# A residual chain of four conditioned layers: the due times of every operation, and thirty unread products, set anew

## The chip, the core and the metric

The kernel runs on one core of one Trainium2 chip. The time is device time in microseconds (us) of one execution; the program is run several times, and the median of the runs is compared. The core has five engines with a queue of instructions each: TensorE (PE, with weight loads shown as PEld), VectorE (DVE), ScalarE (ACT), GpSimd (POOL) and SyncE (SP, which here only issues transfers). Each queue is worked off in its own order; an instruction waits on semaphores for the results that it needs.

## The reference, cut to what matters

The input `x` has 128 sequences of 64 tokens of 256 features in float32, 8192 tokens in all. Four layers are added to it one after the other, each steered by a condition vector of its sequence:

```python
x = x + L0(x, cond)   # keys = values = queries = modulated linear of x; per token, softmax over
                      # the 16 heads' 16-wide keys; modulated linear out
x = x + L1(x, cond)   # per-sequence 256->64->256 with relu, and its own residual
x = x + L2(x, ids, …) # layer norms with gathered gains, three small MLPs of the conditions,
                      # concatenation (6*256) @ int_W1, silu, @ int_W2, layer norm
x = x + L3(x, cond)   # per-sequence 256x256 weight of rank 30: x @ (U @ V) + bias
```

The softmax runs over heads within a token, so the scores of a token are 16 x 16. Everything that depends on conditions alone (styles, demodulations, the decoded `U` of rank 30, the bias rows of the three MLPs) is worked out once.

## The kernel before, in words

The tokens are cut into 16 blocks of 512 (8 sequences each), with features on the partitions in most steps. A prologue (`prologue_keys`, `prologue_rest`, block number -1 in the tables) works out what depends on conditions alone. Its loads are those at lines 702 to 709 (`early`, `wk` 704, `idx` 705, `sel` 706, `wo` 707, `kbr` 708, `late` 709), 642 and 647 (weights and tables), 842 (`wd`, pieces of `W_dec`); its products are at line 629 (small ones) and 851 (decoding `W_dec`, copied on by DVE at 866 or ACT at 858).

Each block has `attention` and `rest`:

- xsT = xT times the style (POOL, 1097; `xT` is loaded at 1039, the token ids at 1044, their one-hot rows `oh` are made by DVE at 1046).
- For each of two pairs: keys (PE, 1191, 8 matmuls), kxe (DVE 1202, POOL 1213), transposes kT and kV (DVE 1228 and 1245), kR (ACT 1237), v (PE 1256, ACT 1261), scores into `sc` (PE 1276, 128 matmuls), maxima (DVE 1289), mt (ACT 1302), a product (PE 1311), mX (ACT 1321), mE (DVE 1328, 1337), the shift of the scores (PE 1350), exponentials e (ACT 1364), the weighted values (PE 1381, 128 matmuls), ao (DVE 1394), rz (DVE 1402), att (POOL 1405), a turn (PE 1418), osT (DVE 1425).
- The output product (PE 1155) and x1T (DVE 1162, 1173).
- L1: PE 1573 and 1591, DVE 1604, with per-block weights from POOL (1129 to 1143). L2: transposes (PE 1648), statistics (DVE 611, 613), rstd (POOL 619, 621; offset by DVE 1623), normalizations (ACT 1633), transposes (PE 1688, ACT 1693), picks (PE 1699, 1716), the large product (PE 1738, sixteen pieces and two of line 1748, between which other work can go), tanh (ACT 1755), DVE 1758, the second product (PE 1785, DVE 1796). L3: PE 1823, 1842, 1867, DVE 1874, output by SP at 1883. The last block ends in `finish` (lines 1447 to 1557), which works in halves.

PSUM is divided into one tile `sc` of four banks and four single banks, which nearly every product takes and gives back when its result was read.

The order on each engine is not that of the program text. Every operation is recorded in a plan with a due time, and the plan is emitted by due time as far as dependences and free buffers allow:

```python
def turns(blk, k):                                   # line 573
    return max(blk, 0) * TURN + tables[blk][k]
...
o["prio"] = self.turns(o["blk"], o["k"])             # in Plan.order
...
o = ops[heappop(ready)[1]]                           # the ready operation that is due first
```

`TURN` is 881500 in units of 1/20000 us, that is 44.1 us from block to block, so work of three or four blocks is interleaved on each engine. `TURNS` holds one table of due times for the prologue and one for each block. The plan also decides which slot of a buffer kind, and which PSUM bank, an operation gets.

The prologue's table has more entries than the prologue has operations. What is left over becomes unread products, made by `spin`: a bf16 product of zeros of 128 x 512, whose result nobody reads. It occupies PE and takes a PSUM bank:

```python
def spin():                                          # line 634
    ps = Buf("bank")
    pe(0.215, lambda: nc.tensor.matmul(ps.t, idle[:, :128], idle, start=True, stop=True), [], [ps], n=2)
...
while plan.noted[-1] + 1 < SPINS:                    # line 1897; SPINS is the length of the prologue's table
    spin()
```

Before, there are 23 of them: 7 at the start, 4 ahead of the last block's product of line 1573, 7 in `finish` behind line 1447, and 5 by themselves.

Of the kernel before, what the change touches and what calls it, by code (L numbers as in the profile page):

```python
# [66 lines left out]
class Plan:  # L67
# [98 lines left out]
    -652225 -652207 -501809 -501797 549383 103302 97834 98988 -85347 -290328 36942 -280951 36928 -327022 -327038  # L166
    -295554 -34519 99192 -93568 76051 -488538 -331376 250663 -320110 311371 -544127 -297616 224193 -331358 437866
    369544 404601 258598 475097 427655 312750 413551 304934 313766 312765 477842 -325751 561445 451452 460137 631735
    653018 914561 435225 761948 708892 413433 313012 683513 477384 477856 415801 449087 706556 405021 840033 397966
    837121 677936 790176 413437 1085501 936816 1219990 374944 1127563 -488523 52290 364768 79632 -329221 31806 69353  # L170
    -302391 37394 74911 -302398 -135690 103317 253823 37375 113108 263257 -19093 -550935 407657 459732 455180 631946
    302035 554215 632190 302064 695445 435656 1285010 1313672 -271895 459095 641073 632445 439004 715974 662881
    443771 715988 735063 451708 763102 706553 455767 763114 790156 408270 1002127 1127290 1030643 1260783 1163421
    1039496 1260792 1322499 1326714 1592341 1603338 1296229 962570 1143817 400034 1095103 400034 1114596 1105723
    370540 1181851 589031 1073580 1215404 1215398 420508 1317621 426029 1244494 1155098 517782 411678 1318626
    1221030 487418 1289492 1063938 409314 1219811 414916 1426329 1505888 1316718 425996 578876 1307095 1544800
    1509955 1509945 1500478 1779993 1762953 1714110 1556735 1872029 1343778 1433951 1901071 1540726 1505870 1355549
    1749223 1065262 1886158 1894341 1920839 1713830 1294728 1463917 2023267 2025009 2024993 1769125 2080980 1991910
    1476886 1764730 2069423 1404270 2200384 1433935 1923896 1907021 2044892 1919551 2192488 1893429 2159446 1342047
    1346981 1402219 2313495 2045469 2494753 2285999 2271380 2543401 2525610 1728898 1728909 2630317 2592995 1746037  # L180
    2451743 1728921 2595973 1718576 1277644 2062908 2395255 316359 450207 16049267 16049281 14504150 -291503
    11290964 2389482 -291825 16049286 -291820 14522440 16049266 16053420 -320001 13567795 -410994 14513815 -361547
    15405911 16048186 16073369 -309973 14522440 16005249
    """,
    0: """
    -484581 84372 -652203 -35682 684863 1289506 1005368 578863 1258365 2419509 2111364 2061858 1597541 357479
    -327047 377451 733801 366553 -328204 806711 387288 365083 406034 1377907 1111313 1160718 1672215 -332266 56194
    404606 447219 455369 431572 -15187 267150 595783 567747 302041 312750 629212 662899 609068 653445 312737 466428
    715978 309121 309112 857128 436276 489161 370548 806701 1063944 1120732 641246 410676 725568 436305 410648
    709812 410662 609042 1119259 602370 436294 477217 820104 818673 1002143 818654 1083255 1103114 1063941 1120265  # L190
    1117581 1073560 1181852 1168792 409321 1262701 1205334 414910 1357801 1505886 426004 1063898 411662 1462748
    1518640 1230468 1433890 1749255 1749239 1431873 1872425 2190164 1919575 1872422 2174910 2278764 2321415 2384852
    2430654 2088493 2292286 2543835 2599889 2409496 1589520 2271367 2543830 2512135 1803634 1326310 2714126 1751071
    1758943 1758957 1758947 2523186 1589506 2427752 2206922 2711663 1788133 2711694 1788156 2575469 2528666 2544499
    2733360 2898539 2917556 2711682 2568763 2598822 2598852 2711679 2711696 2733311 2598849 2781651 2986041 2354176
    2409591 2568757 2598832 2711671 2711680 2733358 2733329 2733335 2985571 2986044 2476838 3049866 2529124 3019122
    3049851 2529112 3092405 3152898 3152886 2477574 3204028 3204039 2342116 2350219 3160743 3160731 2697860 3153889
    3310393 3353979 3296818 3367447 3109127 3394993 3420441 3762300 1336203 3409996 1469597
    """,
    1: """  # L200
    -394079 -394092 -482733 -425615 -297831 -337865 -325537 -299039 -482716 297196 735637 407985 -421370 1532404
# [1818 lines left out]
```

## Time and profile before

| what | value |
|---|---|
| median of 9 runs (lowest, highest) | 824.1 us (816.78, 828.93) |
| profiled execution: time, span | 818.67 us, 816.8 us |
| mean granted TensorE clock over the span | 0.980 |
| busy: PE, PEld | 753.3 us (92%), 488.4 us (60%) |
| busy: DVE, ACT, POOL | 591.4 us (72%), 360.8 us (44%), 565.5 us (69%) |
| transfers | 87.63 MB, mean 107 GB/s |
| queue of instruction loads (q8) | 101 packets, 1.65 MB |

Busy time is the sum over an engine's instructions in one profiled execution. The granted clock is the share of full speed at which TensorE was let run. "Idle before" names the time an engine stood still ahead of an instruction, and what ended it; "issue" means that the profile shows nothing that the engine waited for. The chain of waits is followed back from the last instruction, at each step to what released it.

### The profile page before, as it was taken

Reading aid. Unit: us, or ns where it says so; the run is one execution under the profiler, and the core shown is the slowest. Engines: PE = TensorE matmul, PEld = TensorE weight load, DVE = VectorE, ACT = ScalarE, POOL = GpSimd, SP = SyncE. Lnnn points to the kernel's source line nnn. Section 1 sums busy time; section 2 is a strip of 40 time slices with the busy share of each in tenths; the row PEclk is TensorE's granted clock in tenths of the full one; section 3 lists DMA queues with packets and bytes.
Section 4 is the critical chain, followed back from the end, with each engine's and each line's share of the span. In section 5 each row is a group of like instructions: output and inputs, shape, how many; then the busy total and the mean of one; then the engine's idle time right before and its main releaser. Section 6 shows DMA issues by size and latency. Waiting matters only on the chain.

```text
span 816.8 us, 29440 instructions
## 1 busy us (share of the span) xinstructions
PE 753.3 (92%) x12839; PEld 488.4 (60%) x12843; DVE 591.4 (72%) x1320; ACT 360.8 (44%) x664; POOL 565.5 (69%) x544
## 2 busy tenths in 40 slices
PE   8777889999999999999999999999999989999595
PEld 5655665666666565666666666657566565655353
DVE  4748896968778696969587786869695876866435
ACT  1554345543635362635435353636254353444331
POOL 5453869395868879586869688786779486828243
PEclk9997999999999999999999999999999999999888
DMA  8876742233423244342424333342434232023001
GB/s 269 253 228 205 216 132 85 73 105 107 130 94 81 75 111 119 91 127 85 122 88 107 116 86 106 96 122 68 130 83 123 72 83 63 3 68 99 18 1 53
DMA packets 59297, 87.63 MB, mean 107 GB/s; under 512 B 6456, under 2 KB 42400, under 8 KB 59168
## 3 DMA queue, kind: packets, MB, share of 16 engines
q1 hardware_dynamic: 54048, 68.96, 28.8%
q0 software_dynamic: 5120, 16.78, 7.3%
q8 instruction: 101, 1.65, 0.9%
q14 instruction: 28, 0.23, 0.1%
HBM read 72.48 MB, written 13.24 MB: 105 GB/s over the span
## 4 chain that ended last, share of the span: by engine, by line
PE 61%; DVE 21%; POOL 7%; ACT 5%; issue 4%; DMA 1%; SPq 0%; DVEq 0%; POOLq 0%; ACTq 0%
PE bank L1738 24%; PE bank L1191 6%; PE bank L1785 5%; DVE st L611 4%; DVE mr L1289 4%; PE sc L1276 3%; PE bank L1688 3%; PE bank L1381 3%; PE bank L629 2%; DVE bank L1162 2%; PE bank L1573 2%; PE bank L851 2%; PE bank L1648 1%; PE bank L1823 1%; ACT e L1364 1%
## 5 line engine op out<-in xcount | busy, mean ns | idle before, releaser
L1289 DVE TENSOR_REDUCE mr<-sc 128x16 f32<-128x1024 f32 x64 | 75.7, 1210 | 9.9 <-PE sc L1276 9.9
L1364 ACT ACTIVATE e<-sc 128x1024 f32<-128x1024 f32 x64 | 62.3, 1026 | 33.6 <-PE sc L1350 33.5
L1112 POOL DMA_INDIRECT pw<-in_pw,idx x64 | 65.3, 1021 | 16.0 <-issue 8.2
L1155 PE MATMUL bank<-osT,wo 128*128 128x512 f32 x128 | 63.8, 627 | 5.4 <-DVE osT L1425 5.1
L1738 PE MATMUL bank<-uu,w_s 128*128 128x512 f32 x128 | 63.3, 597 | 0.0
L1191 PE MATMUL bank<-wk,xsT 128*128 128x256 f32 x256 | 62.2, 386 | 0.9 <-DVE uu L866 0.5
L1237 ACT ACTIVATE kR<-kT,early 128x1024 f32<-128x1024 f32 x32 | 39.7, 1242 | 50.0 <-DVE kT L1228 50.0
L1738 PE MATMUL bank<-uu,w_t 128*128 128x512 f32 x128 | 61.3, 605 | 0.3 <-ACT uu L1655 0.2
L1738 PE MATMUL bank<-uu,w_h 128*128 128x512 f32 x128 | 61.4, 602 | 0.0
L1738 PE MATMUL bank<-x2T,w_x 128*128 128x512 f32 x128 | 59.9, 593 | 0.0
L1276 PEld LDWEIGHTS sc<-kR,kT 20*64 20x64 f32 x4096 | 47.5, 130 | 20.0 <-ACT e L1364 8.3
L1381 PEld LDWEIGHTS bank<-e,v 64*32 64x32 f32 x4096 | 44.6, 107 | 24.2 <-issue 20.2
L1785 PE MATMUL bank<-w,uu 128*128 128x256 f32 x240 | 55.8, 385 | 2.2 <-DVE uu L1758 2.1
L1276 PE MATMUL sc<-kR,kT 20*64 20x64 f32 x4096 | 52.3, 232 | 4.6 <-ACT e L1364 1.7
L1381 PE MATMUL bank<-e,v 64*32 64x64 f32 x4096 | 51.0, 230 | 5.8 <-issue 5.8
L1191 PEld LDWEIGHTS bank<-wk,xsT 128*128 128x128 f32 x256 | 48.4, 196 | 12.5 <-issue 3.6
L1202 DVE TENSOR_TENSOR kxe<-bank,dmk 128x512 f32<-128x512 f32 x32 | 22.0, 688 | 43.8 <-PE bank L1191 38.5
L1693 ACT COPY uu<-bank 128x512 f32<-128x512 f32 x64 | 36.4, 587 | 36.4 <-PE bank L1688 36.1
L1785 PEld LDWEIGHTS bank<-w,uu 128*128 128x128 f32 x240 | 44.3, 190 | 9.8 <-DVE uu L1758 3.8
L1129 POOL TENSOR_TENSOR wdn<-gdb,late 128x512 f32<-128x512 f32 x32 | 40.6, 1281 | 13.0 <-PE bank L1573 12.0
L1228 DVE STREAM_TRANSPOSE kT<-kxe 128x512 f32<-128x512 f32 x64 | 42.1, 685 | 9.3 <-POOL kxe L1213 9.3
L1213 POOL TENSOR_TENSOR kxe<-kxe,kbr 128x512 f32<-128x512 f32 x32 | 40.8, 1274 | 10.5 <-DVE kxe L1202 10.2
(241 smaller groups left out, 1783.9 us busy)
## 6 DMA issues: line engine op xcount, KB each, us to landing
xT<-in_xT SPq DMA_DIRECT2D x32, 256.0 KB
gdb<-dgdb SPq DMA_DIRECT2D x16, 512.0 KB
ubb<-ugub SPq DMA_DIRECT2D x32, 256.0 KB
wup<-ugub SPq DMA_DIRECT2D x32, 256.0 KB
ids<-in_ids SPq DMA_DIRECT2D x16, 256.0 KB
ud<-uu SPq DMA_DIRECT2D x8, 512.0 KB
uT<-ud SPq DMA_DIRECT2D x16, 256.0 KB
dmk<-demod_k SPq DMA_DIRECT2D x60, 64.0 KB
```

Of the source, the lines that this page charges most:

```text
L1112: lambda tl=tl, n=n: nc.gpsimd.indirect_dma_start(out=pw[tl // 2].t[:, tl % 2, :], out_offset=None, in_=a["pw"], in_offset=bass.IndirectOf ...
L1129: lambda w=w, dp=dp: nc.gpsimd.tensor_tensor(w(), gdb.t[:, :, 0:64], dp, ALU.mult),
L1155: nc.tensor.matmul(ps.t, owT[:, c, bass.ts(oc, 128)], osT.t[:, c, :], start=(c == 0), stop=(c == C - 1))
L1191: nc.tensor.matmul(ps.t[:, bass.ts(l, F)], xsT.t[:, c, mine2].rearrange("p (n l) -> p l n", l=2)[:, l, :], kwT[:, c, :], start=(c == 0), s ...
L1213: lambda: nc.gpsimd.tensor_tensor(kxe.t[:, :, :, 0:D], kxe.t[:, :, :, 0:D], heads(kinds["kbr"][0]).unsqueeze(1).to_broadcast([128, 2, H, D ...
L1228: lambda l=l: nc.vector.transpose(kT.t[:, l, :].rearrange("p (g h t) -> p h g t", h=H, t=QT), kxe.t[:, l, :, :]),
L1276: nc.tensor.matmul(sc.t[64 * c : 64 * c + 64, q, bass.ts(tg, 64)], cut(kT.t)[r, tg // 4, c, tg % 4, :], cut(kR.t)[r, tg // 4, c, tg % 4, : ...
L1289: lambda two=two: nc.vector.tensor_reduce(mr.t[:, two, :], sc.t[:, two, :].rearrange("p q (g n) -> p q g n", g=TG), AX.X, ALU.max),
L1364: lambda k=k: nc.scalar.activation(es[k].t, sc.t[:, 2 * k : 2 * k + 2, :], AF.Exp, scale=0.25),
L1381: nc.tensor.matmul(placed(pr[c].t)[32 * q : 32 * q + 32, l, g, :, :], v.t[r, l, :].rearrange("p (g q d) -> p g q d", g=4, q=4)[:, g, q, :] ...
L1738: lambda ps=ps, w=w, src=src, fc=fc, c=c, n=n: nc.tensor.matmul(ps.t, w.t[:, c, bass.ts(fc, 128)], src.t[:, c, :], start=(n == 0 and c == ...
L1785: nc.tensor.matmul(ps.t[:, bass.ts(l, F)], s2.t[:, c, bass.ts(2 * p + l, 128)], w2.t[:, c, :], start=(c == 0), stop=(c == C - 1),)
```

## The change

Only numbers change: `TURN` stays, the 16 tables of the blocks keep their lengths, and the prologue's table grows from 254 to 261 entries, which makes 30 unread products of 23. All other code is the same, so every other operation is there once, with the same operands.

```diff
 TURNS = {
     -1: """
-    -652225 -652207 -501809 -501797 549383 103302 97834 98988 -85347 -290328 36942 -280951 36928 -327022 -327038
...
+    -677219 -677238 -664467 -664429 538934 -664462 85946 87100 -161988 -331753 -149704 -321377 -161974 -294788
...
     0: """
-    -484581 84372 -652203 -35682 684863 1289506 1005368 578863 1258365 2419509 2111364 2061858 1597541 357479
...
+    -406988 84372 -652203 -27393 684863 1289506 1054617 1026520 1054613 1243452 2073912 1311799 1606077 355488
...
     15: """
...
 }
 SPINS = len(TURNS[-1].split()) if -1 in TURNS else 331
```

Both programs were built, and their queues laid side by side. Without the unread products, so many operations of each engine stand at the same place in its queue as before:

| engine | operations | at the same place | largest move (places) |
|---|---|---|---|
| PE | 851 | 661 | 9 |
| DVE | 894 | 633 | 19 |
| ACT | 640 | 423 | 11 |
| POOL | 532 | 339 | 7 |
| SP | 348 | 167 | 13 |

Most moves are an exchange of two neighbours, such as two of the sixteen pieces of line 1738, two of the four normalizations of line 1633, or the two transposes of line 1394. The places that are more than that:

- SP at the start. Before: early, aff weights (642), ids, wk, idx, int_W2 (827), xT, three wd, xT, kbr, late, seqs, o_aff weights, demod_k, wo. After: aff weights, early, wk, **wo**, idx, int_W2, **ids**, xT, three wd, xT, kbr, late, seqs, o_aff weights, demod_k. Block 1's xT (1039) goes ahead of later pieces of `W_dec`, small tables and a demodulation store.
- DVE at the start: the one-hot rows `oh` of block 0 (1046) go from ahead of the two style additions (725) to behind the addition of line 742.
- Block 0, pair 1. POOL: line 1213 goes ahead of block 1's two multiplications of line 1097. PE, around the shift of pair 0 (1350): before, a decoding (851), shift, decoding, block 1's keys (1191), scores of pair 1 (1276); after, a decoding, shift, decoding, decoding, scores of pair 1, block 1's keys. ACT: before, a decoding's copy (858), two exponentials (1364), kR of pair 1 (1237); after, a copy, two exponentials, a second copy, kR.
- Block 1, pair 0. DVE: mE (1328, 1337) goes ahead of additions 662 and 687 of the prologue's tables, block 2's `oh` ahead of it. ACT: the prologue's copy of line 903 goes from ahead of the exponentials to behind them, and kR of pair 1 three places forward.
- POOL in the middle blocks: the making of the next blocks' wdn and wup (1129 to 1143), the gathers (1112), rstd (619, 621), kxe (1213) and att (1405) change places among each other.
- Unread products: 7 at the start as before; 7 in place of 4 ahead of the last block's line 1573; 8 in place of 7 in `finish`; 8 single ones in place of 5. Of the single ones the new places are: ahead of block 0's second keys; ahead of block 6's first line 1381; ahead of block 10's line 1155; between two pieces of block 12's line 1738 and its line 1688; and behind block 12's second line 1748, ahead of line 1785. The one ahead of block 3's keys and the one ahead of a shift (1350) of block 12 are gone.

## The prediction

> **What bounds the kernel now.** I read the page's busy times, then the stretches of the span, then the chain of waits, then PE's own waits. The page:
>
> ```profile
> PE 753.3 (92%) x12839; PEld 488.4 (60%) x12843; DVE 591.4 (72%) x1320; ACT 360.8 (44%) x664; POOL 565.5 (69%) x544
> PE 61%; DVE 21%; POOL 7%; ACT 5%; issue 4%; DMA 1%; SPq 0%; DVEq 0%; POOLq 0%; ACTq 0%
> ```
>
> PE carries the kernel; it stands still for 816.8 - 753.3 = 63.5 us. Where, is in the stretches (length, PE, PEld, DVE, ACT, POOL, granted clock, DMA share, GB/s):
>
> ```profile
> 0.00:140.00 140.00, 113.09 (x2028) 83.22 (x2030) 97.83 (x178) 61.47 (x131) 87.83 (x93) 0.94 0.66 201
> 140.00:740.00 600.00, 580.83 (x10417) 372.85 (x10417) 460.51 (x1048) 276.05 (x491) 443.11 (x414) 1.00 0.33 93
> ...
> 47.00:50.00 3.00, 2.52 (x96) 2.35 (x97) 0.85 (x2) 0.76 (x2) 0.00 (x0) 0.50 0.59 190
> 65.00:74.00 9.00, 8.12 (x35) 6.07 (x27) 8.49 (x9) 3.35 (x11) 7.50 (x6) 0.50 0.84 251
> 771.00:780.00 9.00, 4.05 (x16) 3.18 (x17) 1.91 (x13) 5.57 (x11) 8.30 (x9) 0.50 0.00 0
> ```
>
> PE is idle for 26.9 us up to 140 us, 19.2 us in the 600 us of the middle, and 17.4 us after. The middle runs at full clock; around the prologue's and the tail's standstills the clock is half. In the chain of waits (start, length, what) the longest hole of the prologue is this, with two more behind:
>
> ```profile
> 43.52 0.56 PE bank L1381 x37
> 44.08 3.40 issue
> 47.48 1.57 PE bank L1381 x85
> ...
> 59.74 1.11 issue
> ...
> 63.02 1.66 issue
> ```
>
> PE stops between two of the 128 matmuls of one operation, for which nothing in the kernel is awaited, while the transfers are at 0.97 of their capacity or over (44 to 47 us). I take it that the next instructions had not arrived: 3.40 + 1.11 + 1.66 = 6.17 us. Half clock follows each time. What half clock costs is seen in the same operation twice, and beside it an exponential that scores wait for:
>
> ```profile
> 70.98 5.28 PE L1155 MATMUL bank<-osT,wo 128*128 128x512 f32 x8
> 78.74 0.48 PE L1276 MATMUL sc<-kR,kT 20*64 20x64 f32 x30 [1.73 <-ACT e L1364]
> 105.47 3.70 PE L1155 MATMUL bank<-osT,wo 128*128 128x512 f32 x8 [0.89 <-DVE osT L1425]
> ```
>
> PE's waits in the middle (us in total, times, longest):
>
> ```profile
> PE bank L1155 <- DVE osT L1425: 4.2, 9, 0.9
> PE bank L1688 <- DVE ao L1394: 3.9, 8, 1.0
> PE bank L1688 <- DVE x1T L1173: 1.3, 2, 1.0
> ```
>
> They are many and short. A new order of the middle can gain only from such crumbs.
>
> **The change, part by part.** The sum is made against the profiled execution, 818.67 us: span 816.8, 1.9 around it. It lies 5.4 us under the median of 824.1 us, so it is one of the better executions; I apply the sum to the median.
>
> *Start: +0.5 us.* wo (256 KB) is now issued ahead of xT, wd and late, where it was behind them; ids (256 KB) stays ahead of them. At the 296 GB/s of 5 to 13 us that is 262144 B / 296 GB/s = 0.9 us later for those loads. PE's decoding at 9.31 us already waits 0.58 us for wd (in PEld's row), POOL's 1097 waits 0.99 and 2.01 us for xT, DVE's 866 waits 1.87 us for late: no slack. SP's demodulation store, which waits for DVE, stands at the same place, so nothing is newly queued behind it. Against that, wo's old slot behind the store is free (0.43 us of SP), and the second small product with dmk now precedes the style product that stood idle 0.46 us. The moved oh (0.49 us) gains little: the second style addition needs PE's product, modelled to end at 5.24 us, and began at about 5.3. So 0.9 - 0.4 = +0.5; bounds -0.5 and +0.9.
>
> *Block 0, pair 1: +1.0 us.* kxe (POOL 1213, 34.11 us) no longer stands behind two multiplications of 1.02 us and comes about 1 us earlier. But kR, which the scores wait for at 39.52 us (1.09 us), did not start for want of kT: ACT was busy, with a copy of 1.26 us (35.31), then the exponentials (36.34 to 38.20). Now a second copy of 1.26 us stands between them and kR, so kR would end at 40.7 in place of 39.5. Meanwhile PE has a decoding (1.0) where it had block 1's keys (1.9) to fill in. Shift to scores: before 35.5 + 1.1 + 1.9 + 1.09 idle = 39.5. After 35.5 + 1.1 + 1.0 = 37.6, then about 3.1 idle. PE is up to 2.0 us later behind the group. The hole of 3.40 us that follows can swallow all of it, if the instructions arrive when they did. Bounds 0 and +2.0; I take the middle.
>
> *Block 1, pair 0: -0.6 us.* mE no longer stands behind 1.48 + 1.47 us of DVE work, but PE's 1155 runs until 76.2 us anyway, so at half clock this gains nothing. The exponentials at 76.88 us waited for kR (75.67, 1.21 us), and that for the copies and tab (74.83); with those out of the way they start at the shift, 0.3 us earlier. At full clock 1155 ends 5.28 - 3.70 = 1.58 us earlier, and the edit gains what it opens: 0.3 + 1.6 = 1.9. Bounds -1.9 and 0.
>
> *Middle: -1.9 us.* Most moves exchange pieces of sums on PE and cost nothing: the sixteen pieces of 1738 follow each other without idle time (0.0 to 0.3 us per group), and no matmul is added or dropped but the unread ones. What can move is PE's waits there, some 16 us by name. No row says which end. Bounds: half of them gone (-8), or the bank waits of 1688 doubled (+3.9), since the banks are dealt out anew. I take -1.9, an eighth of 16 us with a minus sign, because the stretch has only 3% idle and a re-dealing shifts waits rather than ends them.
>
> *Unread products: +0.4 us.* One costs (0.81 - 0.38) / 2 = 0.215 us (three of them take 0.81 at 737.45, the last 0.38). Of the new ones, three stand ahead of 1573, which waits 1.49 us for x1T at 740.01: covered, and 0.6 us if x1T came at once. Those ahead of block 10's 1155 (0.26 idle), block 12's 1785 (1.01 idle) and block 0's keys (0.52 idle) lie in waits. Those ahead of block 6's 1381 and block 12's 1688 lie in none: behind the first are queued the 128 matmuls and then a 1688 that already waits 0.88 us for their reader. 2 x 0.215 = +0.4; bounds 0 and 7 x 0.215 = +1.5. The tail's 6.51 us without PE work ahead of 1688 at 774.95 us gets none, so its half clock stays.
>
> Sum: +0.5 + 1.0 - 0.6 - 1.9 + 0.4 = -0.6 us: 818.1 us in an execution like the profiled one, **823.5 us** for the median.
>
> **Two rules of the Trainium skill, against the rows.** The 3.40 us hole with the transfers at capacity reads as instructions that come late. "Runtime: NRT & Kernel Launch", Instruction fetch mechanics, says that the fetch is mostly hidden, because dispatch is slower than the fills. By the page, rating orders over fetch delays is worth 0 of the 6.17 us; by the rows, up to all of it. Half of the 2.52 + 8.12 + 4.05 us of PE work in the three half-clock stretches above is 7.3 us, more than a measurement's uncertainty. "TensorE: Matmul & The Clock Gate", The HAM clock gate, says that the gate's window runs free of the kernel's start and that one should not fit the ramp, as it costs under 1% of a typical span. By the page a search over phases is worth nothing that lasts; by the rows up to 7.3 us.
>
> **Rivals.**
>
> *Faster: the prologue's holes close.* If the new order keeps PE out of the holes at 59.74 and 63.02 us, the 1.11 + 1.66 = 2.8 us and the half clock after them go. That stretch has 8.12 us of PE work; by the 1155 rows it saves 8.12 x (1 - 3.70/5.28) = 2.4, by halves 4.1. Together 5.2 to 6.9, with the -0.6: **818.3 us**. For it: the median lies 5.4 us above the profiled execution, so such stretches come and go, which an order rated over phases can use. Against: the same matmuls pass there, at the same places of PE's queue but for a few.
>
> *Slower: a second hole like that of 44 us.* Transfers are more crowded early (wo), PE later by 0.5 to 2 us, and blocks of instructions are asked for at another time. If one block comes late by another 3.40 us between 60 and 100 us, where the transfers are at 0.60 and 0.72 (each 20 us), the hole itself and 2.4 us of half clock come on top: -0.6 + 5.8, **829.3 us**. It decides once a hole exceeds about 2.3 us (2.3 + 2.4 - 0.6 = 4.1). For it: three such holes exist. Against: none beyond 1.7 us after 48 us.
>
> *The change does nothing on the path.* Moves lie in slack, unread products cost 0.4: **824.5 us**.
>
> **How the numbers follow.** About 0.5% (4.1 us) is what a measurement of this kernel can tell from no change, with executions 12 us apart. Forecast 0.38, nothing on the path 0.10, holes close 0.28, second hole 0.24. The forecast's own range is 819 to 828, a spread of its unknown terms; 0.03 of its 0.38 lies below 820.0. So faster 0.28 + 0.03 = 0.31, same 0.35 + 0.10 = 0.45, slower 0.24. The range reaches past both rivals: down to 815, where holes close by halves (823.5 - 6.9 = 816.6) and the middle gives 1.6 more; up to 831, the second hole and half the bank waits' 3.9. About 0.1 is left out on either side.
>
> **What would show it.** Start: the decoding at 9.31 us moves to about 10. Pair 1: the scores' wait for kR (1.09 us) grows towards 3, or vanishes into a hole of 3.4. Block 1: the 1.73 us ahead of the scores shrinks. Middle: PE idle between 140 and 740 us is 17 to 18 us for 19.2. I am wrong if "issue" holes in matmul groups of the prologue change by over 2 us in sum, or if the middle's idle time changes by over 4 us.

## The result, and the profile after

| kernel | median (lowest, highest) of runs | ratio to before |
|---|---|---|
| before | 825.34 us (816.78, 833.24), 62 runs | 1 |
| changed | 835.88 us (825.78, 839.22), 20 runs | 1.0116, 95% interval 1.0093 to 1.014 |

The changed kernel is slower, by some 9.6 us on 824.1. The forecast was 823.5 us with a range of 815 to 831: wrong in sign. The ratio is taken between the faster executions of both kernels, without those over 1.5% above the fastest of their kernel, so it is not exactly that of the medians. The profiled execution took 830.17 us (span 828.4 us, mean granted clock 0.973).

The page after, busy times and shares of the chain of waits (in the changed kernel every line number is one higher):

```profile
PE 756.3 (91%) x12844; PEld 491.4 (59%) x12850; DVE 587.4 (71%) x1320; ACT 360.0 (43%) x664; POOL 565.8 (68%) x544
PE 56%; DVE 22%; POOL 7%; ACT 7%; issue 4%; DMA 2%; SPq 1%; POOLq 0%; ACTq 0%; DVEq 0%
```

PE's share of the chain fell from 61% to 56%; ACT, DMA and DVE rose by 1 to 2 points each. The stretches (length, PE, PEld, DVE, ACT, POOL, granted clock, DMA share, GB/s):

```profile
0.00:140.00 140.00, 106.90 (x2003) 82.36 (x2004) 88.12 (x161) 57.99 (x124) 78.55 (x84) 0.89 0.64 191
140.00:740.00 600.00, 579.93 (x10405) 370.27 (x10406) 454.32 (x1031) 275.50 (x491) 447.01 (x416) 1.00 0.34 95
```

PE is idle for 33.1 us up to 140 us (26.9 before) and for 20.1 us in the middle (19.2 before). Between these two executions nearly all of the loss falls ahead of the first output: its store is issued at 184.6 us where it was at 173.8, and the last store at 822.4 where it was at 811.3. Where, is in PE's timeline (start, length, operation, idle time before it and what ended it), first of the kernel before, around the scores of pair 1, then of the changed kernel:

```profile
34.12 1.16 PE L851 MATMUL bank<-early,wd 128*128 128x128 f32 x8 [1.54 <-DVE mE L1337]
35.21 0.40 PE L1350 MATMUL sc<-mE,sel 32*128 32x512 bf16 x4
35.53 1.16 PE L851 MATMUL bank<-early,wd 128*128 128x128 f32 x8
36.53 1.90 PE L1191 MATMUL bank<-wk,xsT 128*128 128x256 f32 x8
39.52 1.59 PE L1276 MATMUL sc<-kR,kT 20*64 20x64 f32 x128 [1.09 <-ACT kR L1237]
```

```profile
10.17 5.29 PE L852 MATMUL bank<-early,wd 128*128 128x128 f32 x24 [1.77 <-DMA wd<-in_W_dec]
...
39.22 2.07 PE L852 MATMUL bank<-early,wd 128*128 128x128 f32 x8 [2.71 <-DMA wd<-in_W_dec]
41.23 0.61 PE L1351 MATMUL sc<-mE,sel 32*128 32x512 bf16 x4
41.77 3.78 PE L852 MATMUL bank<-early,wd 128*128 128x128 f32 x16
47.91 1.69 PE L1277 MATMUL sc<-kR,kT 20*64 20x64 f32 x128 [2.36 <-ACT kR L1238]
...
74.89 0.49 PE L1277 MATMUL sc<-kR,kT 20*64 20x64 f32 x7 [5.52 <-issue]
...
87.39 1.59 PE L1277 MATMUL sc<-kR,kT 20*64 20x64 f32 x128 [1.62 <-ACT e L1365]
```

The scores of pair 1 start at 47.91 us where they started at 39.52. Ahead of them are a wait of 2.71 us for a piece of `W_dec` that was not there before, and one of 2.36 us for kR. Behind them, at 69.36 us, comes a hole of 5.52 us in the middle of an operation, where the kernel before had holes of 3.40, 1.11 and 1.66 us between 44 and 65 us. PE's operations are also longer: the two decodings at 41.77 us take 3.78 us, where two together take 2.05 at full clock (18.10 us, before). From 15 to 60 us the granted clock is 0.85, where it is 0.96 before. Why kR is late is seen in ACT's timeline, first of the kernel before, then of the changed one:

```profile
29.93 1.25 ACT L858 ACTIVATE uu<-bank,late 128x128 f32<-128x128 f32 x4 [0.23 <-PE bank L851]
...
32.61 0.31 ACT L1321 ACTIVATE mX<-bank,early 128x64 bf16<-128x64 f32 x1 [0.96 <-PE bank L1311]
32.94 1.28 ACT L807 ACT_TABLE_LOAD   x1
...
35.31 1.26 ACT L858 ACTIVATE uu<-bank,late 128x128 f32<-128x128 f32 x4 [0.78 <-PE bank L851]
36.34 2.00 ACT L1364 ACTIVATE e<-sc 128x1024 f32<-128x1024 f32 x2
38.20 1.26 ACT L1237 ACTIVATE kR<-kT,early 128x1024 f32<-128x1024 f32 x1
```

```profile
36.55 0.31 ACT L1322 ACTIVATE mX<-bank,early 128x64 bf16<-128x64 f32 x1 [2.76 <-PE bank L1312]
36.76 1.24 ACT L859 ACTIVATE uu<-bank,late 128x128 f32<-128x128 f32 x4
38.00 1.28 ACT L808 ACT_TABLE_LOAD   x1
...
41.33 1.25 ACT L859 ACTIVATE uu<-bank,late 128x128 f32<-128x128 f32 x4 [1.73 <-PE bank L852]
42.36 1.98 ACT L1365 ACTIVATE e<-sc 128x1024 f32<-128x1024 f32 x2
45.59 1.25 ACT L859 ACTIVATE uu<-bank,late 128x128 f32<-128x128 f32 x4 [1.25 <-PE bank L852]
46.62 1.24 ACT L1238 ACTIVATE kR<-kT,early 128x1024 f32<-128x1024 f32 x1
```

From mX to kR ACT needed 5.6 us (32.61 to 38.20); it now needs 10.1 (36.55 to 46.62). Not one but two more copies of decodings have come between. The first of them stood in ACT's idle time ahead of mX (29.93 us) and now follows it, ahead of the table load; the second follows the exponentials, and it waits 1.25 us itself, because it belongs to the last of three decodings on PE. Of the 4.5 us, 2.1 lie ahead of the exponentials (the first copy, and a wait of 1.73 us instead of 0.78 for the decoding that comes late) and 2.4 behind them (the second copy with its wait).

### The profile page after: what moved, and what is told of

The parts are those of the page before. It is cut to its first block, busy times and chain, and to the rows that moved or that the text cites. A ratio compares the mean times of both kernels' runs of the same rounds, so it can differ in the third digit from the quotient of the medians.

```text
span 828.4 us, 29449 instructions
## 1 busy us (share of the span) xinstructions
PE 756.3 (91%) x12844; PEld 491.4 (59%) x12850; DVE 587.4 (71%) x1320; ACT 360.0 (43%) x664; POOL 565.8 (68%) x544
## 4 chain that ended last, share of the span: by engine, by line
PE 56%; DVE 22%; POOL 7%; ACT 7%; issue 4%; DMA 2%; SPq 1%; POOLq 0%; ACTq 0%; DVEq 0%
PE bank L1739 21%; PE bank L1192 6%; PE bank L1786 4%; DVE st L612 4%; DVE mr L1290 4%; PE sc L1277 3%; PE bank L1689 3%; PE bank L852 2%; PE bank L1382 2%; PE bank L630 2%; ACT e L1365 2%; DVE bank L1163 2%; PE bank L1574 2%; PE bank L1649 1%; PE bank L1824 1%
## 5 line engine op out<-in xcount | busy, mean ns | idle before, releaser
L1192 PE MATMUL bank<-wk,xsT 128*128 128x256 f32 x256 | 65.5, 401 | 0.3 <-ACT v L1262 0.2
L1192 PEld LDWEIGHTS bank<-wk,xsT 128*128 128x128 f32 x256 | 50.8, 205 | 13.3 <-issue 6.0
L1406 POOL TENSOR_TENSOR p<-ao,rz 128x512 f32<-128x512 f32 x14 | 14.8, 1055 | 54.4 <-DVE rz L1403 54.4
```

The source lines that it names most:

```text
L1192: nc.tensor.matmul(ps.t[:, bass.ts(l, F)], xsT.t[:, c, mine2].rearrange("p (n l) -> p l n", l=2)[:, l, :], kwT[:, c, :], start=(c == 0), s ...
```

## The experiments

Ratios are to the unchanged kernel on the same chip, with their 95% intervals; 0.1% is 0.8 us. The chips differ: the unchanged kernel's median is 824.1 to 825.6 us on two of them, as in the series ahead of the prediction, and 832.6 to 833.2 us on three others. So ratios can be compared across chips, and starts and spans of single profiled executions only with care.

### First cuts: due times of one part exchanged

Apart from the first, the eight kernels of this part took the due times of some operations from one version and the rest from the other. The plan then emits by due time, so operations whose due time was left alone can move too.

**The unchanged kernel against itself.** No edit.

> The kernel before once more, unchanged, against itself, so that the interval and a second trace of it on this chip can be read. Every theory: a ratio of 1.000, interval within 0.004 of it. Its trace on this chip should show fewer waits on PE before 140 us than the kernels with parts of the change, if the parts really cost in the prologue; with the same waits, the parts' losses are a matter of the single execution.

Measured 0.9984 (0.9952 to 1.0016). Its profiled execution has a span of 833.2 us, where the first had 816.8 us. It ran on a chip where the kernel's median is 833.2 us, and it stands still and slows down at other places:

```profile
0.00:140.00 140.00, 109.52 (x2016) 82.03 (x2017) 94.81 (x173) 59.16 (x126) 84.48 (x90) 0.91 0.64 197
140.00:740.00 600.00, 577.48 (x10258) 369.73 (x10257) 449.81 (x1016) 272.61 (x487) 441.35 (x410) 0.99 0.33 94
```

PE is idle for 30.5 and 22.5 us in these stretches, where the first execution had 26.9 and 19.2, and the first output's store is issued at 178.6 us, where it had 173.8. So two executions of one kernel, on chips of different medians, differ by 3 to 4 us in each, as much as the effects that I had predicted from one execution.

**Changed kernel, SP's due times of the prologue and blocks 0 to 3 as before.**

```diff
-    SP of blocks -1 to 3: due times of the changed kernel
+    SP of blocks -1 to 3: due times of before
```

> The changed kernel, in which the due times of SP's transfers in the prologue and blocks 0 to 3 are those of before; PE, DVE, ACT and POOL keep the changed order. Loads theory: the loss comes from transfers that were moved (wo ahead of xT and wd; later pieces of W_dec behind block 1's xT), so most of it goes: a ratio of about 1.002 to the kernel before, PE's waits for wd (1.8 us at 10 us, 2.7 us at 39 us) disappear. Queue theory: the loss comes from the orders of ACT, DVE, POOL and PE in the prologue, so the ratio stays at about 1.011 and the wait for kR of 2.4 us stays. Middle theory (blocks 4 to 15 and unread products): 1.011.

Measured 1.0107 (1.0071 to 1.0143).

**The kernel before, only SP's due times of these blocks changed.**

```diff
-    SP of blocks -1 to 3: due times of before
+    SP of blocks -1 to 3: due times of the changed kernel
```

> The kernel before, in which only SP's transfers of the prologue and blocks 0 to 3 have the changed due times; the other engines and the unread products stay. Loads theory: slower by about 8 us, a ratio of 1.010, with waits for wd of 2 to 3 us on PE at the start. Queue theory: 1.000 to 1.002, that is at most the 0.9 us by which 256 KB more stand ahead of xT and wd. Middle theory: 1.000.

Measured 1.007 (1.0035 to 1.0106).

**The kernel before, all five engines' due times of the prologue and blocks 0 to 3 changed.**

```diff
-    PE, DVE, ACT, POOL, SP of blocks -1 to 3: due times of before
+    PE, DVE, ACT, POOL, SP of blocks -1 to 3: due times of the changed kernel
```

> The kernel before, with the changed due times of the prologue and blocks 0 to 3 on all engines; blocks 4 to 15 and the unread products stay. Loads theory and queue theory both: 1.010 to 1.012, the block outputs late by 8 to 10 us from 115 us on. Middle theory: 1.000 to 1.003.

Measured 1.011 (1.0061 to 1.0159): the due times of the prologue and the first four blocks are enough for a loss of this size.

**The kernel before, blocks 4 to 15 changed.**

```diff
-    all engines, blocks 4 to 15: due times of before
+    all engines, blocks 4 to 15: due times of the changed kernel
```

> The kernel before, with the changed due times of blocks 4 to 15 alone; the prologue, blocks 0 to 3 and the unread products stay. Loads theory and queue theory: 0.998 to 1.002, since the traces of the two kernels run apart by only about 1 us between 115 and 690 us. Middle theory: 1.008 to 1.012.

Measured 1.0033 (1.0004 to 1.0062): +2.7 us (0.3 to 5.1), a loss where I had a gain of 1.9. These blocks include the tail.

**The kernel before, wo right behind wk and ids behind int_W2.**

```diff
 SP: early, aff weights,
-    ids, wk, idx, int_W2, xT, 3 wd, xT, kbr, late, seqs, o_aff, demod_k, wo
+    wk, wo, idx, int_W2, ids, xT, 3 wd, xT, kbr, late, seqs, o_aff, demod_k
```

> The kernel before with one transfer moved: wo stands right behind wk, and the ids behind int_W2, as in the changed kernel; all else as before. Loads theory: most of what SP's changed order cost alone (0.7%), so 1.004 to 1.007, with PE's decoding at 9.3 us later by 0.9 us and a wait for wd there. Later-loads theory (the cost of SP's order lies in the pieces of W_dec at 30 to 40 us): 1.000 to 1.001. Fragile-prologue theory (any change there moves PE's holes and half clock): 1.003 to 1.010, with no wait of 0.9 us that explains it.

Measured 1.0026 (0.999 to 1.0062), unclear. The edit was half of what belongs together: DVE's one-hot rows (1046) still stood ahead of the style additions, waited 3.78 us for the later ids, and PE stood behind them, as PE's timeline of this kernel shows:

```profile
10.52 2.08 PE L629 MATMUL bank<-p,p 128*128 128x256 f32 x4 [5.29 <-POOL p L735]
```

The SP-only kernel above has the same wait (5.90 us). In the changed kernel it is 2.14, as before, since there the one-hot rows have moved too.

**The kernel before, PE's, DVE's, ACT's and POOL's due times of the prologue and blocks 0 to 3 changed.**

```diff
-    PE, DVE, ACT, POOL of blocks -1 to 3: due times of before
+    PE, DVE, ACT, POOL of blocks -1 to 3: due times of the changed kernel
```

> The kernel before with the changed due times of PE, DVE, ACT and POOL in the prologue and blocks 0 to 3; SP's transfers, blocks 4 to 15 and the unread products as before. Loads theory: 1.000 to 1.004. Queue theory: 1.007 to 1.011, with a wait of the scores for kR of 2 to 3 us near 45 us. Fragile-prologue theory: 1.004 to 1.010, and the place of the loss differs from that of the changed kernel.

Measured 1.0145 (1.0101 to 1.0188).

**The kernel before, only ACT's due times of these blocks changed.**

```diff
-    ACT of blocks -1 to 3: due times of before
+    ACT of blocks -1 to 3: due times of the changed kernel
```

> The kernel before with ACT's changed due times in the prologue and blocks 0 to 3 alone. Queue theory with the second copy ahead of kR as its step: 1.003 to 1.006 and the wait for kR of 2 to 3 us. If the queue theory holds but its step lies on another engine: 1.000 to 1.002 and a wait for kR of about 1 us as before. Fragile-prologue theory: 1.003 to 1.010 with or without that wait.

Measured 1.0343 (1.0297 to 1.0389). These last two, and the first with SP's due times as before, do not tell what they were made for. In all three the plan moved kbr and late behind the demodulation store, which waits for DVE. In the kernel with four engines changed, late was issued at 13.10 us instead of 6.4, and the trace shows who paid (SP, DVE, PE):

```profile
13.10 0.46 SPq L709 DMA_DIRECT2D late<-in_late  x1
```

```profile
19.66 1.89 DVE L866 TENSOR_TENSOR uu<-bank,late 128x512 f32<-128x512 f32 x3 [7.43 <-DMA late<-in_late]
```

```profile
20.50 3.75 PE L1191 MATMUL bank<-wk,xsT 128*128 128x256 f32 x8 [5.25 <-DVE uu L866]
```

Neither version has this wait of PE. From here on I fixed the queues themselves.

### Second cuts: every queue given place by place

The order of emission now comes from a table of ranks, the merge of five written-out queues; the choice of buffer slots still goes by due times. With a version's own queues this reproduces that version's order and slots.

```diff
-            o["prio"] = self.turns(o["blk"], o["k"])
+            o["prio"], o["rank"] = self.turns(o["blk"], o["k"]), RANK[o["blk"]][o["k"]]
...
-        ready = [(o["prio"], o["n"]) for o in ops if not o["wait"]]
+        ready = [(o["rank"], o["n"]) for o in ops if not o["wait"]]
```

**The group of block 0's pair 1 alone, in the kernel before.** d1, d2, d3 are the three decodings in the order of their loads, c1 to c3 their copies.

```diff
 PE:
-    d1, shift, d2, keys of block 1, scores of pair 1, a small product, d3
+    d3, shift, d2, d1, scores of pair 1, keys of block 1, a small product
 ACT:
-    c1, e, e, kR, c2, ..., c3
+    c3, e, e, c1, kR, c2, ...
 POOL:
-    1097, 1097 of block 1, 1213 of pair 1
+    1213 of pair 1, 1097, 1097 of block 1
```

> The kernel before with one group of queue places as in the changed kernel and every other place of every queue as before: around the shift of block 0's pair 0, PE takes the decoding of the piece that is loaded third first, then the shift, then the decodings of the pieces loaded second and first, then the scores of pair 1 and only then block 1's keys; ACT's copy of the last of these decodings stands between the exponentials and kR; POOL's 1213 of pair 1 stands ahead of block 1's two 1097. Group theory: PE waits 2 to 3 us for a piece of W_dec (line 851) at about 37 us and 2 to 3 us for kR (line 1237) at about 44 us, where the kernel before waits 0 to 1.1 us; the time is 2 to 4 us longer, ratio 1.002 to 1.005. Transfer theory (the moved loads are the loss): neither wait is over 1.5 us, ratio 0.998 to 1.002. Theory of the holes (late instructions and half clock decide wherever they fall): the waits are there, the ratio is 0.998 to 1.002 because a hole behind the group swallows them.

Measured 1.005 (1.0013 to 1.0088); the waits are 2.52 us for the piece and 2.36 us for kR. Both waits are as the group theory has them, and the ratio is at the upper end of its range.

**The same, and the earlier copy behind mX.**

```diff
 ACT (on top of the run before):
-    mt, 858, 795, mt, mX, table load
+    mt, 795, mt, mX, 858, table load
```

> The kernel before with the group (first run of the group) and, besides, the copy of the earlier decoding (line 858) moved from ACT's idle time between the two mt copies to behind mX, as in the changed kernel; all other places as before. Chain theory: the wait for kR grows by up to 1.25 us over the 2.36 us of the group alone, the ratio is 1.005 to 1.009. If the chain is hidden behind the wait for the piece of W_dec: the wait for kR stays at 2.4 us and the ratio at 1.003 to 1.006.

Measured 1.0057 (1.0025 to 1.0088). In PE's timeline:

```profile
43.94 2.26 PE L1276 MATMUL sc<-kR,kT 20*64 20x64 f32 x128 [2.97 <-ACT kR L1237]
```

The wait for kR grows by 0.6 us (2.36 to 2.97), not by 1.25, and that for the piece shrinks from 2.52 to 1.96; the two runs can't be told apart in time.

**Changed kernel, kR ahead of the second copy.**

```diff
 ACT:
-    e, e, 858, kR
+    e, e, kR, 858
```

> The changed kernel with one place of ACT's queue undone: kR of block 0's pair 1 (line 1237) goes ahead of the copy of the decoding (line 858) that the changed kernel puts between the exponentials and kR; all other places are the changed kernel's. Group theory: the wait of the scores of pair 1 for kR, 2.36 us in the changed kernel, falls under 0.5 us, the wait of 2.7 us for a piece of W_dec ahead of the shift stays, and the ratio to the kernel before is 1.008 to 1.010 where the changed kernel has 1.0116. Transfer theory and theory of the holes: the wait falls too, the ratio stays at 1.011 to 1.012.

Measured 1.0104 (1.0054 to 1.0154). The wait for kR falls to 0.39 us, as said; the time can't tell 1.009 from 1.0116 here.

**Changed kernel, kR ahead of the copy and the decodings in the order of their loads.**

```diff
 PE:
-    d3, shift, d2, d1
+    d1, shift, d2, d3
 ACT:
-    c3, e, e, c1, kR
+    c1, e, e, kR, c3
```

> The changed kernel with two places undone: kR of block 0's pair 1 goes ahead of the copy as in the run before, and the decodings of the pieces loaded first and third, with their copies, change places, so that PE takes the pieces in the order of their loads. Group theory: both waits (2.36 us for kR, 2.71 us for the piece) fall under 1 us, the scores of pair 1 start 3 to 5 us earlier than the changed kernel's 47.9 us, and the ratio to the kernel before is 1.005 to 1.008. Transfer theory: the wait for the piece stays over 2 us, because all pieces are late, ratio 1.009 to 1.012. Theory of the holes: the waits fall, the ratio stays at 1.010 to 1.012.

Measured 1.0087 (1.0047 to 1.0126). In PE's timeline:

```profile
39.75 0.40 PE L1351 MATMUL sc<-mE,sel 32*128 32x512 bf16 x4 [0.59 <-DVE mE L1338]
40.07 2.05 PE L852 MATMUL bank<-early,wd 128*128 128x128 f32 x16
45.39 2.12 PE L1277 MATMUL sc<-kR,kT 20*64 20x64 f32 x128 [3.26 <-ACT kR L1238]
```

The wait ahead of the shift for the piece is gone, but a wait of 3.26 us for kR is back and the scores start at 45.39 us, 2.5 earlier instead of 3 to 5. PE comes earlier and finds ACT's chain, lengthened by the first copy, still running.

**Changed kernel, SP's whole queue as before.**

```diff
 SP, all blocks:
-    places of the changed kernel
+    places of the kernel before
```

> The changed kernel with SP's whole queue exactly as before (kbr and late ahead of the demodulation store, wo behind it, block 1's xT behind the pieces of W_dec), the other four engines' queues exactly the changed kernel's. Transfer theory: the ratio to the kernel before falls to 1.000 to 1.004, and the waits for late (3.75 us on DVE) and for W_dec (1.77 and 2.71 us on PE) fall under 1.5 us. Group theory: the wait for kR stays at 2 to 4 us and the ratio at 1.006 to 1.011; only the waits of the first 15 us fall. Theory of the holes: the ratio stays at 1.010 to 1.014.

Measured 1.0108 (1.0056 to 1.016). The waits for the piece (3.13 us) and for kR (2.36 us) stay. The piece is late because it is asked for out of order, not because its load has moved. The transfer theory falls: the scores of pair 0 start at 25.50 us, as early as before, and the ratio stays.

**The start alone, in the kernel before** (SP's first 17 places, the one-hot rows on DVE, the small product on PE).

```diff
 SP:
-    early, aff weights, ids, wk, idx, int_W2, xT, 3 wd, xT, kbr, late, seqs, o_aff, demod_k, wo
+    aff weights, early, wk, wo, idx, int_W2, ids, xT, 3 wd, xT, kbr, late, seqs, o_aff, demod_k
 DVE:
-    1046, 725, 725, 742
+    725, 725, 742, 1046
 PE:
-    style product, keys, second product with dmk
+    second product with dmk, style product, keys
```

> The kernel before with the start of the changed kernel alone: SP's first 17 transfers in the changed order (wo and ids where the changed kernel has them), the one-hot rows (DVE 1046) behind the style additions, and the second small product with dmk ahead of the style product; every other place of every queue as before. By the prediction's first term (+0.5 us, bounds -0.5 to +0.9) the decoding (PE 851) starts at about 10.2 us, and the ratio is 0.999 to 1.002. If the loads of the start are the loss, the decoding starts after 11 us and the ratio is 1.005 or more.

Measured 1.0022 (0.9986 to 1.0058); the decoding starts at 9.75 us.

**The unread products alone, in the kernel before.**

```diff
-    23 unread products at the places of before
+    30 unread products at the places of the changed kernel
```

> The kernel before with the unread products of the changed kernel at the changed kernel's places (30 in place of 23), all other operations of every queue in the order of before. By the prediction's fifth term (+0.4 us, bounds 0 to +1.5) the ratio is 1.000 to 1.002. If the unread products, which also take PSUM banks and so deal out the banks anew, are a main part of the loss: 1.004 or more.

Measured 0.9995 (0.9964 to 1.0026).

**Changed kernel, the group as before.**

```diff
 PE, ACT, POOL around block 0's pair 1:
-    d3, shift, d2, d1, scores, keys | c3, e, e, c1, kR, mt, c2 | 1213, 1097, 1097
+    d1, shift, d2, keys, scores, d3 | c1, e, e, kR, c2, c3, mt | 1097, 1097, 1213
```

> The changed kernel with the whole group of block 0's pair 1 as before: the three decodings, block 1's keys and the scores on PE, the copies, exponentials and kR on ACT, 1213 and 1097 on POOL. If the parts add up (group alone 1.005 in the kernel before, whole change 1.0116): the waits for kR and for the piece of W_dec fall under 1.5 us each and the ratio is 1.005 to 1.008. If another queue change of the prologue brings the same delay without it (the parts do not add up): 1.009 to 1.012.

Measured 1.0075 (1.0041 to 1.011), as adding up would have it. But the wait for kR stays at 2.42 us where it was to fall under 1.5: the first copy was still behind mX.

**The same, and blocks 4 to 15 as before.**

```diff
 all engines, blocks 4 to 15:
-    places of the changed kernel
+    places of the kernel before
```

> The run before (changed kernel with the group as before) with the operations of blocks 4 to 15 in the order of before on every engine as well. If the parts add up (group 1.005, middle and tail 1.0033, start 1.0026 or less): 1.001 to 1.005. If they do not: 1.007 or more, and the loss sits in the places of the first four blocks that are left changed.

Measured 1.0136 (1.0092 to 1.018). The parts do not add up here: taking the middle's order back costs more than keeping it (medians of 842.96 and 839.14 us on the same chip). By its expectation the loss then sits in those places of the first four blocks, outside the group, that are still changed. Which of them, and why the old order of blocks 4 to 15 loses behind them, was not tried.

**Changed kernel, ACT's chain cleared.**

```diff
 ACT:
-    mt, mt, mX, 858, table load, wsm, c3, e, e, c1, kR
+    mt, 858, mt, mX, table load, wsm, c1, e, e, kR, c3
 PE:
-    d3, shift, d2, d1
+    d1, shift, d2, d3
```

> The changed kernel with ACT's chain from mX to kR of block 0's pair 1 cleared: the copy of the decoding ahead of it (line 858, the first of the group) goes back into ACT's idle time between the two mt copies, kR goes directly behind the exponentials, and the decodings are taken in the order of their loads. Chain theory (two copies of 1.25 us stand between mX and kR, and a piece of W_dec is asked for in the wrong order): exponentials start 1.2 us earlier behind mX than the changed kernel's 5.8 us, the wait for kR is under 1.5 us, that for the piece under 1.5 us, the scores start within 5 us of the shift (6.7 us in the changed kernel), and the ratio to the kernel before is 1.005 to 1.008. If the chain is not the loss: waits fall as said, the ratio stays at 1.010 or more.

Measured 1.0053 (1.0023 to 1.0084); this interval lies below that of the changed kernel (from 1.0093). The timelines of ACT and PE:

```profile
38.49 0.31 ACT L1322 ACTIVATE mX<-bank,early 128x64 bf16<-128x64 f32 x1 [0.60 <-PE bank L1312]
...
43.20 1.26 ACT L1238 ACTIVATE kR<-kT,early 128x1024 f32<-128x1024 f32 x1
```

```profile
39.99 0.40 PE L1351 MATMUL sc<-mE,sel 32*128 32x512 bf16 x4 [0.59 <-DVE mE L1338]
...
44.51 1.81 PE L1277 MATMUL sc<-kR,kT 20*64 20x64 f32 x128 [2.14 <-ACT kR L1238]
```

From mX to kR ACT needs 4.7 us, less than the 5.6 of the kernel before. The wait for kR, 2.14 us, missed its number (under 1.5): the keys that used to fill PE's time still stand behind the scores. The distance from the shift to the scores is 4.52 us here, 6.68 in the changed kernel.

### Side by side

Starts on PE in us, from one profiled execution each (first decoding; scores of pair 0; shift; scores of pair 1), the time from shift to scores, and the ratio measured:

| kernel | decoding | scores 0 | shift | scores 1 | shift to scores 1 | ratio |
|---|---|---|---|---|---|---|
| before, first execution | 9.31 | 25.43 | 35.21 | 39.52 | 4.31 | 1 |
| before, second execution | 9.69 | 27.09 | 38.48 | 43.28 | 4.80 | 0.9984 |
| before + unread products | 9.40 | 25.81 | 37.29 | 41.61 | 4.32 | 0.9995 |
| before + start | 9.75 | 26.23 | 36.95 | 41.26 | 4.31 | 1.0022 |
| before + group | 9.26 | 25.25 | 37.93 | 43.33 | 5.40 | 1.005 |
| before + group + first copy | 9.27 | 25.48 | 38.60 | 43.94 | 5.34 | 1.0057 |
| changed | 10.17 | 29.27 | 41.23 | 47.91 | 6.68 | 1.0116 |
| changed, SP as before | 8.73 | 25.50 | 37.88 | 44.38 | 6.50 | 1.0108 |
| changed, kR ahead of the copy | 9.39 | 28.25 | 41.20 | 45.52 | 4.32 | 1.0104 |
| changed, kR ahead and decodings in order | 9.95 | 29.01 | 39.75 | 45.39 | 5.64 | 1.0087 |
| changed, group as before | 9.61 | 28.89 | 37.68 | 43.31 | 5.63 | 1.0075 |
| changed, group and blocks 4 to 15 as before | 10.47 | 29.27 | 40.02 | 45.66 | 5.64 | 1.0136 |
| changed, chain cleared | 10.04 | 29.11 | 39.99 | 44.51 | 4.52 | 1.0053 |

The last distance follows ACT's chain. It is 4.3 to 4.8 us in the kernels whose chain is as before or cleared. It is 5.3 to 6.7 us where a copy stands between the exponentials and kR, and 5.6 us in three kernels where kR directly follows the exponentials but the first copy still stands behind mX. The exception is the kernel with kR alone put back (4.32 us): there the piece taken out of order holds up the shift itself, so ACT has caught up by then.

But the distance is not the whole price. That same kernel has 4.32 us and a ratio of 1.0104, and the one with blocks 4 to 15 as before has 5.64 us and 1.0136. What goes along with the changed order of the first blocks, and what I left out, is the clock (stretch from 15 to 60 us of before, its second execution, and the changed kernel):

```profile
15.00:60.00 45.00, 34.92 (x685) 28.66 (x686) 25.68 (x45) 23.19 (x53) 23.16 (x21) 0.96 0.81 257
15.00:60.00 45.00, 35.08 (x575) 28.26 (x582) 26.21 (x45) 22.30 (x50) 22.12 (x20) 0.96 0.80 252
15.00:60.00 45.00, 34.11 (x544) 28.76 (x543) 24.36 (x43) 19.26 (x46) 16.95 (x17) 0.85 0.66 208
```

The granted clock (third figure from the end) is 0.96 to 1.00 there in the first five rows of the table. It is 0.89 with the first copy added, and 0.77 to 0.89 in every row from the changed kernel on. An estimate of what 0.85 costs against 0.96 is at most 0.11 x 45 = 5.0 us of full-speed work, as much as the group. No run separates this lower clock from the waits that it comes with.

## Why the prediction was wrong, by its own steps

**Start, +0.5 (bounds -0.5 to +0.9): the mechanism was right, the size is open.** The decoding was to move to about 10 us and started at 10.17, waiting 1.77 us for `wd`. Alone, the start gives 1.0022, +1.8 us with -1.2 to +4.8.

**Block 0, pair 1, +1.0 (bounds 0 to +2.0): the mechanism was right, the size was not.** This is the step that failed: its measure lies outside its own bounds. Measured alone with the first copy it is 1.0057, +4.7 us (2.1 to 7.3); with ACT's chain cleared and the decodings in order in the changed kernel, the ratio falls from 1.0116 to 1.0053, 5.2 us. I saw kR behind one more copy of 1.26 us and missed three things. The copy that stands there belongs to the last decoding of the three, so it waits for PE (1.25 us in the trace) before it begins. The decodings were "a decoding" each to me, but the one that now comes first is loaded third, and PE waits 2.71 us for it where it waited 1.54 for mE. And ACT's first copy moved from idle time to behind mX, which I did not list and did not price. It lengthens the chain from mX to kR by 1.1 us (5.8 with kR ahead and the decodings in order, 4.7 cleared); its share of the time is not shown (1.005 without it, 1.0057 with it). I also put no price on half clock behind the new waits. "The hole can swallow all of it" did not happen: a hole of 5.52 us came behind it.

**Block 1, pair 0, -0.6 (bounds -1.9 to 0): not measured, and no gain is seen in the trace.** The 1.73 us ahead of its scores became 1.62, though the product of line 1155 ran at full clock there (3.65 us, at 81.36, where it had taken 5.28), where I had expected 1.9 from the edit. I did not run this edit by itself.

**Middle, -1.9 (bounds -8 to +3.9): the sign was wrong.** Alone, blocks 4 to 15 are +2.7 us (0.3 to 5.1), a miss of 4.6 us, though inside the bounds. PE's waits there changed their names rather than went away:

```profile
PE bank L1689 <- DVE ao L1395: 2.7, 4, 0.9
PE bank L1574 <- DVE ao L1395: 2.1, 1, 2.1
...
PE bank L1689 <- ACT uu L1634: 1.7, 3, 0.7
PE bank L1689 <- ACT p L1634: 1.6, 3, 0.7
```

Of DVE's rows, osT went from 4.2 us to 1.8 and ao at line 1688 from 3.9 to 2.7 (first line here), but a single wait of 2.1 us for ao is new, ahead of line 1573 (second line). ACT's two, which were 0.4 and 0.3, are 1.7 and 1.6. The idle time went from 19.2 to 20.1 us, not to 17 to 18; the second execution of before has 22.5. "A re-dealing shifts waits rather than ends them" was in the text, and I took a minus sign all the same.

**Unread products, +0.4 (bounds 0 to +1.5): right as far as can be measured.** 0.9995 is -0.4 us, from -3.0 to +2.1.

The four terms that were measured alone add up to 4.7 + 2.7 + 1.8 - 0.4 = 8.8 of 9.6 us. That this is a full account is not shown: only the intervals of the group and the middle exclude no change, the prologue's part with blocks 0 to 3 alone gave 1.011 already, and with the group and the middle both taken back the ratio was 1.0136. What is shown is that the places around block 0's pair 1 carry about half of the loss. Put into the kernel before (with the keys behind the scores and POOL's order) they cost 4.7 us, and clearing ACT's chain and the order of the decodings in the changed kernel takes back 5.2. How much of this is waiting and how much is lower clock, and how the rest divides, stays open.

**The rivals.** "Faster: the prologue's holes close" did not come: "issue" time on PE up to 140 us is 7.4 us in the first execution of before, 11.2 in its second, and 7.0 in the changed kernel, so it says more about the execution than about the order. "Slower: a second hole" named the right sign, and its cause is not borne out: the hole of 5.52 us lies at 69 us, in its window and over its point of decision, but the two kernels that differ from the changed one only around kR and in the group have none over 2.52 us (4.2 and 4.0 us in sum up to 140 us), with ratios of 1.0104 and 1.0075. And the kernel before with the unread products has two of 2.7 us, at 59.83 and 64.75 us, and 11.3 us in sum, with 0.9995. What the hole adds to the one execution that has it is open. The sign that I gave for being wrong, a change of over 2 us in the "issue" holes, is met by the unchanged kernel against itself (3.8 us) and not by the changed one (0.4 us), so it was no test. "Half clock follows each time" was misread too: from 60.85 to 63 us, behind the hole of 1.11 us, the clock is 1.00.

**The two rules.** "Runtime: NRT & Kernel Launch", Instruction fetch mechanics, would have the fetch mostly hidden. Holes of up to 5.52 us, and of 7 to 11 us in sum up to 140 us, would not be hidden if they are late instructions; whether they are was not tried. "TensorE: Matmul & The Clock Gate", The HAM clock gate, says not to fit the ramp, because the window runs free of the kernel's start. The two executions of before fit that: the granted clock of the first 140 us is 0.94 in one and 0.91 in the other, with the same instructions. But the ramp at the start is not all: in the profiled executions the clock from 15 to 60 us goes with the order of the queues, 0.96 twice before and 0.85 changed.

## What to carry to other kernels

When an instruction is put in front of one that is waited for, price it at the time when it can end, its own wait included, and follow the engine's chain back to the last point where that engine was idle; moving an instruction out of idle time is an edit, and it lengthens the chain that it joins. Instructions that look alike are not alike if their loads come one after the other: write down which load each needs. To take an order apart, fix each queue place by place, since a list scheduler moves what was left alone; and take two executions of the same kernel, on the same chip, before building a sum from the differences within one. A short local wait is not yet a short kernel: the ratio decides.

## What was not expected of the hardware

One kernel has a median of 824.1 to 825.6 us in three series and of 832.6 to 833.2 us in three others, on different chips. Its two profiled executions, one from either group, differ by 16.4 us in span (816.8 and 833.2 us), and about 9 us of that is the distance between the two medians. "Issue" holes and stretches of lower clock lie at different places: in the first 140 us PE is idle for 26.9 us in the one and 30.5 us in the other. Against that, the time between two operations that an engine's queue ties together repeats to 0.02 us: 4.30 to 4.32 us from the shift to the scores in six executions of six kernels (three of the table, three of the first cuts) that share ACT's order there and differ in start, middle, transfers or unread products (4.80 in the one where PE was slowed at this place). A distance of this kind is a better measure of a local edit than the idle time of a whole stretch.
